# A second Strassen step in the q product of an attention block, with its statistics on another engine

## The chip, the cores and the metric

The kernel runs on one core of a Trainium2 chip. The metric is the device time of one execution in microseconds (us): 2830.47 us is the median of three runs before the change (2829.81 to 2830.92).

Five engines matter. TensorE multiplies matrices; the profile calls it PE, and its weight loads PEld. VectorE is DVE, ScalarE is ACT, GpSimd is POOL, and SyncE (SP) issues most transfers. SBUF is the memory that all of them read; PSUM holds what PE writes, in eight banks of 128 partitions by 512 float32 numbers. All data here is float32, and PE then leaves two records (instructions) for each multiply.

## The reference

Eight samples of 512 channels by 1024 positions go through two layers.

```python
# layer 0: group norm (32 groups), 8 heads of 64 channels
qkv = einsum('oc,bchw->bohw', qkv_w, group_norm(x)) + qkv_b
attn = softmax(einsum('bhnd,bhmd->bhnm', q, k) / sqrt(64))
x = x + proj_w @ (attn @ v) + proj_b
# layer 1: one norm over the whole sample, one head of 512 channels
n = (x - mean(x)) * rsqrt(var(x) + eps) * gamma + beta
q, k, v = wq @ n + bq, wk @ n + bk, wv @ n + bv
attn = softmax(q^T k * 512**-0.5)
x = x + wo @ (v @ attn^T) + bo
```

## The kernel before

**Algebra.** In layer 1 the kernel multiplies the weights beforehand: `wqk1` is wk transposed times wq, `wvo1` is wo times wv, each scaled by gamma on its way in. So a sample needs one product "q" (512 by 512 times 512 by 1024), one product "v", scores against x itself, and values. The norm is not applied to x (`untaken`, L350): q is scaled per row by gamma, gets a per-row term `norm.c` that holds mean and deviation, and the softmax gets a factor.

**Strassen.** Large products are done in Strassen's form with seven products instead of eight (`strassen`, L414): A11 B11, A12 B21, S1 T1, S2 T2, S3 T3, A22 T4, S4 B22, where S1 to S4 are sums of weights' quarters and T1 to T4 are differences of the moving operand's quarters (`Combined.make`, L394, one DVE operation of 128x1024 each). A "line" bank in PSUM takes A11 B11, S2 T2, S3 T3 and A22 T4 one upon the other; ACT copies it out in between. A "single" bank takes the other three. Some products get a second step (`by_two_steps`, L545, in layer 0's q and k and in layer 1's v): the products A12 B21, S1 T1, S4 B22 and A22 T4 are themselves done in seven, on quarters of quarters, for two row blocks together. Their weights' sums are made once (`WeightTwice`, L514), stored in DRAM and loaded for each sample by ACT's queue; the moving sums of a quarter are three DVE operations (`quarters_b`, L504: one of 128x512, L494, and two of 128x256, L500).

**Order.** For PE, ACT and DVE the order of instructions is the order of the program (`manual_schedule`), written out by hand: a generator yields after each step of PE, `together` (L607) alternates two generators, and `at_steps` (L619) calls the hooks of a step after it. POOL and SP are ordered by the framework. Tiles come from pools: 36 tiles of 128x1024 in SBUF, and in PSUM two tiles each of the tags "s" and "o", each of two banks; a new tile waits until the last reader of an old one is done.

**One sample** takes about 347 us of PE. The stages around the change are:

1. Layer 0's scores and values, in 64 units, then q and k of the next sample (`pairs_qk_twice`, L846). Its hooks divide layer 0's output by the softmax's sums: steps 18 and 19 call `divide_at` (L1108), which is `divide` (L978, one DVE operation of 128x512, L980). There are two head pairs ("couple") and two halves of the positions for each. T1 of the projection needs both halves of a pair; the second product needs both pairs' first halves.
2. The projection, `project` (L1211) in `layer0`: plain Strassen, two generators c = 0, 1 in turn, ten steps. `done` adds PSUM and the copy (L1231), adds bias and x into x (L1217), and calls `norm.of_half` (L318, a DVE statistics operation, 128x512). Four aggregates follow (L321).
3. The q stage, `make_q` (L1288) in `attention1`: plain Strassen, ten steps of PE. DVE adds (L1292), ACT scales by gamma and adds `norm.c` (L1296). Hooks make T1 to T4 of x (L400), the halved quarters of B21, T1, B22 and T4 (`halve_b`), and the norm: `mean_of_all` (L325) is a small PE product that averages over partitions (L299), a reduction (L301) and three small DVE operations (L329 to L333); `deviation` (L335) is a second small product and a power on POOL (L339). ACT's queue issues the load of `wvo1`'s sums (L523, L524).
4. The v stage (`make_v_twice`), then scores, softmax and values of layer 1.

Before the samples there is a prologue, in which weights are multiplied, scaled by gamma (`scale_rows`, L232, on ACT) and summed (`finish`, L186, L194).

The projection's second product reads what DVE divides in hooks 18 and 19 of the stage before it, and its T1 is finished there too (`combine2`, L1030):

```python
18: [lambda g=g: divide_at(couple[0], g) for g in range(2)],
19: [
    lambda: divide_at(couple[1], 0), lambda: combine2(1, 1),
    lambda: divide_at(couple[1], 1),
],
```

Of the kernel before, what the change touches and what calls it, by code (L numbers as in the profile page):

```python
# [37 lines left out]
FP = mybir.dt.float32  # L38
AF = mybir.ActivationFunctionType
# [7 lines left out]
P = 128  # L47
# [18 lines left out]
def two_attention_blocks(  # L66
# [12 lines left out]
    vectors: bass.AP,  # L79
    out: bass.AP,  # L80
# [118 lines left out]
    class Weight:  # L199
# [36 lines left out]

        def finish(self):
            for parts, rest in zip(self.parts, self.rest):
                finish(parts, rest)
            stored[self.name] = dram.tile([P, W_SIZE], FP, tag=self.name, name=f"stored_{self.name}")  # L240
            nc.sync.dma_start(stored[self.name], self.tile)
# [62 lines left out]
    class Norm:  # L304
# [19 lines left out]

        def mean_of_all(self):  # L325
            self.mean = self.average(self.stat[:, 0, :], f"m_{self.name}")
            spread = self.spread = self.tile("spread", NC)
            if self.width == 1:
                nc.vector.tensor_scalar(spread, self.stat[:, 0, :], self.mean, None, ALU.subtract)  # L329
            else:  # L330
                nc.vector.tensor_tensor(spread, self.stat[:, 0, :], self.mean, ALU.subtract)
            nc.vector.tensor_tensor(spread, spread, spread, ALU.mult)
            nc.vector.tensor_tensor(spread, spread, self.stat[:, 1, :], ALU.add)  # L333
# [177 lines left out]

    PAIRS = [[("A12", "B21"), ("S1", "T1")], [("S4", "B22"), ("A22", "T4")]]

    class WeightTwice:  # L514
# [3 lines left out]
        def __init__(self, name, make=None):  # L518
# [7 lines left out]
            for n, pair in enumerate(PAIRS):  # L526
                for i, (a, _) in enumerate(pair):
                    sums_a(self.quarters(a, make), tiles[n][:, i * 4 * P : (i + 1) * 4 * P])
            stored[key] = dram.tile([P, 16 * P], FP, tag=key, name=f"stored_{key}")
            for n in range(2):  # L530
                nc.sync.dma_start(stored[key][:, n * 8 * P : (n + 1) * 8 * P], tiles[n])
# [375 lines left out]
    def layer0(bs, qs, ks, b, norm_next):  # L907
# [5 lines left out]
        if norm_next is not None:  # L913
            for n in range(NC):
                hooks[n + 4] = [lambda cc=n, half=half: norm_next.of_half(cc, half) for half in range(2)]
            hooks[8] = [lambda cc=cc: norm_next.of_channels(cc) for cc in range(NC)]
        twice_b = {}
# [264 lines left out]
        if not last:  # L1182
# [12 lines left out]
                18: [lambda g=g: divide_at(couple[0], g) for g in range(2)],  # L1195
                19: [
                    lambda: divide_at(couple[1], 0), lambda: combine2(1, 1),
# [11 lines left out]
        later = []  # L1209

        def project(w, c):  # L1211
            def done(i, half, bank, u):
# [3 lines left out]
                def add():  # L1216
# [3 lines left out]
                    norm.of_half(chunk, half)  # L1220
# [29 lines left out]
        at_steps(  # L1250
            together(project(w, 0), project(w, 1)),
            {} if last else {2 * n - 3: [lambda n=n: combine2(n, 1)] for n in range(2, 5)},
        )
        for cc in range(NC):
            norm.of_channels(cc)
        if last:
            held(invs.pop(end), f"inv_0_{b}_{end}_1")
        return xs, norm, qs_next, ks_next

    def attention1(xs, norm, b, at_values):  # L1260
# [11 lines left out]
        w = next_weight().parts[0]  # L1272
        twice_w = []
        combine, later = Combined(f"1_{b}"), []
        combine.take(xs)
# [3 lines left out]
        twice_a, twice_b = {}, {}  # L1279
# [5 lines left out]
        def halve_b(name):  # L1285
            twice_b[name] = quarters_b(bs[name], tile2(f"{name}_twice_{b}"))

        def make_q(c):  # L1288
            def done(i, half, bank, u):
                n, to = c + 2 * i, piece(qs, c + 2 * i, half)  # L1290
                if u is not None:
                    nc.vector.tensor_tensor(u, bank, u, ALU.add)  # L1292
                    bank = u

                def scaled():
                    nc.scalar.activation(  # L1296
                        to, bank, AF.Identity, bias=norm.c[:, n : n + 1],
                        scale=vec[:, V_NW1 + n : V_NW1 + n + 1],
                    )

                if i == half == 0:
                    later.append(scaled)
                else:
                    scaled()

            return strassen(by_channels(w, c, bs), done, f"q_1_{b}_{c}")

        at_steps(together(make_q(0), make_q(1)), {
            0: [lambda: combine.make(1)],
            1: [lambda: combine.make(2)],  # L1310
            2: [norm.mean_of_all, lambda: combine.make(3)],
            3: [lambda: halve_b("B21")],
            4: [norm.deviation, lambda: combine.make(4)],
            6: [lambda: halve_b("T1")],
            7: [lambda: halve_b("B22")],
            8: [lambda: halve_b("T4")],
            5: [lambda: twice_w.append(WeightTwice("wvo1")), norm.untaken, lambda: later.pop(0)(), lambda: later.pop(0)()],
# [395 lines left out]
    made, throughs = {}, []  # L1713


    with tc.manual_schedule(engines={PE, ACT, DVE}):
# [12 lines left out]
        norm = norm0(xs_next, 0)  # L1729

# [23 lines left out]
        def through_q():  # L1754
            throughs.append(Through(wqk1, bias_q, nk1, "q", room("rows_q", 0)))
            wqk1.scale_rows(V_NW1)

        def channels_of(half, ccs):
# [25 lines left out]
            7: [wqk1.finish], 8: [waiting[0].finish], 9: [lambda: WeightTwice("qk02", both_of(w))],  # L1784
# [4 lines left out]
        for b in range(B):  # L1789
            if 0 < b < B - 1:  # L1790
                ahead = [norm0(load_x(b + 1, nc.sync), b + 1)]
            xs, norm, qs, ks = layer0(bs, qs, ks, b, ahead[0] if b + 1 < B else None)
# [15 lines left out]
            attention1(xs, norm, b, at_values)  # L1808
# [412 lines left out]
```

## Time and profile before

| | |
|---|---|
| median of 3 runs | 2830.47 us (2829.81 to 2830.92) |
| the profiled execution: its time | 2829.01 us |
| its span, first to last instruction | 2827.3 us |
| ACT busy, POOL busy | 1101.6 us, 273.7 us |
| DVE busy in the projection (939.2 to 963.8 us) and in q (963.8 to 988.3 us) of one sample | 17.78 and 18.90 us |
| ACT busy in the same two stretches | 3.52 and 8.61 us |

The profile is one execution. A row names the line, the engine, the operation, what it writes and reads, the shape and the count; then the time busy and the mean of one in ns; then the idle time of its engine before it and what ended that. A row of the view in order of time begins with the start in us and the length. Consecutive matmuls overlap in the records, since their length includes the way through the array: the distance of two starts is what one costs. The chain that ended last is followed back from the last instruction, at each step to what released it.

### The profile page before, as it was taken

What the parts mean: (1) busy time and instruction counts of PE and PEld (TensorE: products, weight loads), DVE (VectorE), ACT (ScalarE), POOL (GpSimd) and SP (SyncE); (2) the same over time, 40 slices, a digit from 0 to 9 for tenths busy, and PEclk for the clock granted to TensorE, in tenths of its full rate; (3) what the DMA queues carried; (4) which work ended last, traced back from release to release, by engine and by line L of the source; (5) the groups of instructions that cost most, each with busy time, mean ns of one, the idle gap of its engine ahead of it and who ended that gap; (6) DMA issues with size and microseconds to landing.
All of it is one profiled execution on the core that took longest, in us unless ns stands there. A gap on an engine that the chain in (4) does not pass through costs nothing.

```text
span 2827.3 us, 38614 instructions
## 1 busy us (share of the span) xinstructions
PE 2814.0 (100%) x15496; PEld 1550.4 (55%) x15496; DVE 2123.9 (75%) x2979; ACT 1101.6 (39%) x1536; POOL 273.7 (10%) x236
## 2 busy tenths in 40 slices
PE   9999999999999999999999999999999999999999
PEld 5434765357643476445773456734567346673365
DVE  6677696767867778776777777777777777767877
ACT  3462324623256232552325522265232642326432
POOL 0000220003100040000400004000040000400011
PEclk9999999999999999999999999999999999999999
DMA  8422131321323213133131331313213142121001
GB/s 288 168 74 89 53 126 64 87 90 53 112 68 91 84 67 105 59 91 109 56 108 44 89 108 56 108 49 96 96 62 103 49 119 72 64 91 52 8 16 39
DMA packets 81125, 237.76 MB, mean 84 GB/s; under 512 B 21513, under 2 KB 22313, under 8 KB 74537
## 3 DMA queue, kind: packets, MB, share of 16 engines
q1 hardware_dynamic: 73336, 208.44, 22.5%
q10 hardware_dynamic: 7600, 26.77, 2.9%
q8 instruction: 124, 2.03, 0.3%
q14 instruction: 65, 0.52, 0.1%
HBM read 179.37 MB, written 31.98 MB: 75 GB/s over the span
## 4 chain that ended last, share of the span: by engine, by line
PE 92%; DVE 6%; issue 1%; ACT 0%; SPq 0%; DMA 0%; POOL 0%; DVEq 0%; ACTq 0%; POOLq 0%
PE s L941 15%; PE ps_o L960 15%; PE ps_q L632 8%; PE ps_v L647 7%; PE ps_o L1540 7%; PE ps_p L632 6%; PE ps_l_qk L869 5%; PE ps_l L1376 4%; PE ps_s L1359 4%; PE ps_s_qk L862 4%; PE ps_l_v L647 3%; PE ps_s L1376 3%; PE ps_o_qk L862 3%; PE ps_s_v L890 2%; PE ps_s_two L1670 2%; PE ps_o_v L890 1%
## 5 line engine op out<-in xcount | busy, mean ns | idle before, releaser
L798 ACT ACTIVATE p<-s 128x1024 f32<-128x1024 f32 x512 | 523.8, 1025 | 329.0 <-PE s L941 322.2
L800 DVE TENSOR_TENSOR acc<-acc,p 128x1024 f32<-128x1024 f32 x384 | 469.6, 1223 | 101.2 <-ACT p L798 93.0
L960 PE MATMUL ps_o<-p,v 64*64 64x512 f32 x4096 | 528.6, 589 | 0.0
L941 PE MATMUL s<-c_q,c_k 64*64 64x512 f32 x3584 | 465.0, 590 | 0.0
L960 PEld LDWEIGHTS ps_o<-p,v 64*64 64x64 f32 x4096 | 156.6, 133 | 282.9 <-issue 278.0
L941 PEld LDWEIGHTS s<-c_q,c_k 64*64 64x64 f32 x3584 | 134.7, 133 | 253.2 <-issue 236.1
L339 POOL TENSOR_TENSOR rstd<-rstd,minus_half 128x4 f32<-128x4 f32 (+1 forms) x16 | 19.8, 1239 | 2076.9 <-DVE rstd L338 2076.9
L1540 PE MATMUL ps_o<-t_p,s_v 128*128 128x512 f32 x384 | 168.2, 594 | 0.0
L800 DVE TENSOR_TENSOR acc<-p,p 128x1024 f32<-128x1024 f32 x64 | 78.3, 1224 | 79.8 <-ACT p L798 79.8
L1350 ACT ACTIVATE p<-p,factor 128x512 f32<-128x512 f32 (+1 forms) x112 | 85.3, 780 | 115.7 <-DVE p L1386 91.2
L1540 PEld LDWEIGHTS ps_o<-t_p,s_v 128*128 128x128 f32 x384 | 72.3, 190 | 91.3 <-issue 89.2
L1364 ACT COPY p<-ps_s 128x512 f32<-128x512 f32 x96 | 53.1, 588 | 177.0 <-PE ps_s L1359 177.0
L1386 DVE TENSOR_TENSOR p<-ps_l,p 128x512 f32<-128x512 f32 x136 | 90.1, 684 | 40.5 <-PE ps_l L1376 40.2
L632 PE MATMUL ps_q<-t,w_wqk 128*128 128x512 f32 x256 | 116.0, 597 | 0.0
L632 PE MATMUL ps_p<-t_p,w_p 128*128 128x512 f32 x256 | 112.6, 592 | 0.5 <-DVE inv L812 0.5
L425 ACT COPY u_v<-ps_v 128x512 f32<-128x512 f32 x48 | 28.1, 586 | 204.9 <-PE ps_v L647 170.5
L1386 DVE TENSOR_TENSOR p<-ps_s,p 128x512 f32<-128x512 f32 x112 | 74.8, 685 | 37.9 <-PE ps_s L1376 37.9
L647 PE MATMUL ps_v<-w_v,t_again 128*128 128x256 f32 x448 | 99.0, 379 | 0.0
L425 ACT COPY u_q<-ps_q 128x512 f32<-128x512 f32 x54 | 31.2, 578 | 160.6 <-PE ps_q L632 160.6
L647 PEld LDWEIGHTS ps_v<-w_v,t_again 128*128 128x128 f32 x448 | 85.1, 190 | 11.6
L632 PE MATMUL ps_p<-o,w_p 128*128 128x512 f32 x192 | 88.5, 597 | 2.3 <-DVE o L980 2.3
L647 PE MATMUL ps_v<-w_v,x 128*128 128x256 f32 x384 | 86.8, 379 | 0.0
(463 smaller groups left out, 4851.1 us busy)
## 6 DMA issues: line engine op xcount, KB each, us to landing
x<-in_x SPq DMA_DIRECT2D x92, 512.0 KB, 6.4
w_qk<-stored_qk SPq DMA_DIRECT2D x14, 1792.0 KB, 7.2
w_wqk<-stored_wqk SPq DMA_DIRECT2D x8, 1792.0 KB, 7.2
fold<-acc SPq DMA_DIRECT2D x56, 256.0 KB, 3.1
qk_twice<-stored_qk_twice ACTq DMA_DIRECT2D x28, 512.0 KB, 5.8
w_wvo<-stored_wvo SPq DMA_DIRECT2D x8, 1792.0 KB, 7.4
out<-x SPq DMA_DIRECT2D x28, 512.0 KB, 4.6
w_v<-stored_v SPq DMA_DIRECT2D x7, 1792.0 KB, 7.0
```

What stands on the lines that cost most here:

```text
L632: nc.tensor.matmul(bank, w[a][:, k, c * P : (c + 1) * P], bs[b][:, k, :], start=fresh and k == 0, stop=k == 1, skip_group_check=True,)
L647: nc.tensor.matmul(bank[:, u * 2 * P : (u + 1) * 2 * P], bs[b][:, k, n * P : (n + 1) * P], w[a][:, k, :], start=fresh and u == k == 0, sto ...
L798: nc.scalar.activation(p, s, AF.Exp, scale=factor)
L800: nc.vector.tensor_tensor(acc, first, p, ALU.add)
L862: nc.tensor.matmul(bank[:, i * 2 * P : (i + 1) * 2 * P], parts[a][x], twice_b[v][y], start=start and i == 0, stop=True, skip_group_check=True,
L869: nc.tensor.matmul(bank, of(i, a)[:, k, :], bs[v][:, k, :], start=start and k == 0, stop=k == 1, skip_group_check=True,)
L941: nc.tensor.matmul(s[cols, j, :], ks[pair][k0 // HALF][rows, k0 % HALF : k0 % HALF + HD], qs[pair][g][rows, :], start=True, stop=True,)
L960: nc.tensor.matmul(o[cols, half, :], vs[kt][rows, c0 : c0 + HD], p[rows, j, :], start=kt == 0, stop=kt == NT - 1,)
L1359: nc.tensor.matmul(bank, bs[v][:, k, t * P : (t + 1) * P], q_parts[a][:, k, :], start=a == "A11" and k == 0, stop=k == 1, skip_group_check ...
L1376: nc.tensor.matmul(bank[:, u * 2 * P : (u + 1) * 2 * P], v[y][:, u * P : (u + 1) * P], a[x], start=start and u == 0, stop=True, skip_group ...
L1386: nc.vector.tensor_tensor(at(r, t), bank, at(r, t), ALU.add)
L1540: nc.tensor.matmul(bank, v_parts[kt // 2][a][:, kt % 2, c * P : (c + 1) * P], p_parts[kt // 2][b][:, kt % 2, cols], start=fresh and kt == ...
```

## The change

1. **Layer 1's q gets the second Strassen step.** For each row block r = 0, 1 the line takes A11 B11, S2 T2 and S3 T3 only; the four other products are done as quarter products, in two pairs: (A12 B21, S4 B22) and (S1 T1, A22 T4). The two lines of A11 B11 stand before and between the first three quarter products.
2. **The weights are scaled by gamma on both sides** in the prologue, by DVE (`scale_both`), so that ACT need not scale q; a new input `gamma1` is loaded as a row to all partitions. The sums for `wqk1` are made in four steps, as hooks of layer 0's v stage of the first sample, stored, and loaded for each sample in the projection's first hook.
3. **Statistics of x by ACT.** `of_half` and `of_channels` go. Each half of a channel chunk gets two passes of ACT that sum over 512 positions: the mean, and the square about the first half's mean. Seven small POOL operations put the two halves together; the three small operations after the mean go from DVE to POOL.
4. **The halvings of B22 and B21** move from the q stage into the projection's last steps.
5. **The quotients' order**: both pairs' first halves at step 18, the second halves at step 19.

```diff
+        def scale_both(self, by, row):
+            for cc in range(NC):
+                for to, a in self.moving(cc):
+                    nc.vector.scalar_tensor_tensor(
+                        a, a, vec[:, by + cc : by + cc + 1], row[:, to], ALU.mult, ALU.mult
+                    )
...
+        def pass_over(self, cc, half, name, func, **args):
+            to = onepool.tile([P, HALF], FP, tag="held", name=f"{name}_{self.name}_{cc}_{half}")
+            nc.scalar.activation(to, piece(self.xs, cc, half), func, **args)
+
+        def moments(self, cc, half, first):
+            mean, part = self.stat[:, 0, cc : cc + 1], self.part[:, cc, 0 if first else 1, :]
+            self.pass_over(
+                cc, half, "mean", AF.Identity, scale=1.0 / HALF,
+                accum_out=mean if first else part[:, 1:2],
+            )
+            self.pass_over(
+                cc, half, "square", AF.Square, bias=mean, scale=-1.0, accum_out=part[:, 0:1]
+            )
+
+        def both_halves(self):
+            mean, var = self.stat[:, 0, :], self.stat[:, 1, :]
+            (q0, q1), d = (self.part[:, :, i, 0] for i in range(2)), self.part[:, :, 1, 1]
+            nc.gpsimd.tensor_tensor(d, d, mean, ALU.subtract)
+            nc.gpsimd.tensor_tensor(q0, q0, q1, ALU.add)
...
         def mean_of_all(self):
             self.mean = self.average(self.stat[:, 0, :], f"m_{self.name}")
             spread = self.spread = self.tile("spread", NC)
+            engine = nc.gpsimd if self.width == 1 else nc.vector
...
+    PAIRS_Q = [[("A12", "B21"), ("S4", "B22")], [("S1", "T1"), ("A22", "T4")]]
...
-                18: [lambda g=g: divide_at(couple[0], g) for g in range(2)],
+                18: [lambda pair=pair: divide_at(pair, 0) for pair in couple],
                 19: [
-                    lambda: divide_at(couple[1], 0), lambda: combine2(1, 1),
+                    lambda: divide_at(couple[0], 1), lambda: combine2(1, 1),
                     lambda: divide_at(couple[1], 1),
                 ],
...
-                    norm.of_half(chunk, half)
+                    if i == half or i == 1:
+                        norm.moments(chunk, half, i == half)
+                    if (i, half, c) == (1, 0, 1):
+                        ready.halve("B21")
...
+        hooks[0] = [ready.load]
+        hooks[7] = [lambda: ready.halve("B22")]
+        at_steps(together(project(w, 0), project(w, 1)), hooks)
-        for cc in range(NC):
-            norm.of_channels(cc)
...
+        def make_q(w):
+            parts = ready.weights.all(columns_of(w))
+            first, second = ([tile2(f"{n}_q_1_{b}_{r}") for r in range(2)] for n in ["c11", "c22"])
+            lines = [banks("o", f"ps_l{r}_q_1_{b}")[:, 0, :] for r in range(2)]
+
+            def pair(products, to, name):
+                line, single = (banks("s", f"ps_{name}{n}_q_1_{b}")[:, 0, :] for n in range(2))
...
+                for bank, x, y, start, use, r, t in [
+                    (line, "A11", "B11", True, nc.scalar.copy, 0, 0),
+                    (single, "A12", "B21", True, add, 0, 0),
+                    (line, "S2", "T2", False, nc.scalar.copy, 0, 1),
+                    (single, "S1", "T1", True, nc.scalar.copy, 1, 1),
+                    (line, "S3", "T3", False, add, 1, 1),
+                    (single, "S4", "B22", False, add, 0, 1),
+                    (line, "A22", "T4", False, nc.scalar.copy, 1, 0),
+                ]:
+                    for i, (a, v) in enumerate(products):
+                        nc.tensor.matmul(
+                            bank[:, i * 2 * P : (i + 1) * 2 * P], parts[a][x], twice_b[v][y],
+                            start=start and i == 0, stop=True, skip_group_check=True,
+                        )
...
+            yield from line(0, "A11", "B11", True)
+            yield from some(quarters, 2)
+            yield from line(1, "A11", "B11", True)
+            for n in range(5):
+                next(quarters)
+                if n == 0:
+                    take(0)
+                if n == 4:
+                    take(1)
+                yield
+            yield from line(0, "S2", "T2", False)
+            yield from line(1, "S2", "T2", False)
+            quarters = pair(PAIRS_Q[1], second, "s")
+            for n in range(7):
+                next(quarters)
+                if n == 2:
+                    c12_of(0)
+                if n == 4:
+                    c12_of(1)
+                yield
...
+            for r in range(2):
+                multiply(r, "S3", "T3", False)
+                for n, half in enumerate([1, 0]):
+                    final(r, 1, half, lines[r], second[r][:, n, :])
+                yield
+
+        at_steps(make_q(w), {
+            1: [lambda: norm.moments(0, 1, False)],
+            2: [lambda: combine.make(1), lambda: norm.moments(1, 1, False)],
+            3: [lambda: combine.make(2), norm.both_halves],
+            6: [lambda: combine.make(4)],
+            8: [lambda: twice_w.append(WeightTwice("wvo1"))],
+            9: [norm.mean_of_all, lambda: ready.halve("T1")],
+            10: [norm.deviation, lambda: ready.halve("T4")],
+            12: [lambda: combine.make(3)],
+            14: [norm.untaken],
         })
...
+        gamma_row = tile2("gamma_row")[:, 0, :]
+        nc.sync.dma_start(gamma_row, gamma1.to_broadcast([P, C]))
...
-            wqk1.scale_rows(V_NW1)
+            wqk1.scale_both(V_NW1, gamma_row)
...
+                lambda: WeightTwice("qk02", both_of(w)), lambda: WeightTwice("wqk1", columns_of(wqk1), over),
```

`add`, `take` (C11), `c12_of` (C12) and `final` are DVE operations of 128x512 that read PSUM and a tile in SBUF, except the two `final` calls after the last quarter products, which read two tiles in SBUF. The list `over` holds the four steps of sums for `wqk1`; layer 0's v stage of the first sample calls them at its steps 0 to 3.

## The prediction

> **What bounds the kernel now.** I read the page's busy times first, then the chain that ended last, then who waited for whom on the matrix engine (PE), then the instructions in order of time around one layer-1 q stage.
>
> ```profile
> span 2827.3 us, 38614 instructions
> PE 2814.0 (100%) x15496; PEld 1550.4 (55%) x15496; DVE 2123.9 (75%) x2979; ACT 1101.6 (39%) x1536; POOL 273.7 (10%) x236
> PEclk9999999999999999999999999999999999999999
> PE 92%; DVE 6%; issue 1%; ACT 0%; SPq 0%; DMA 0%; POOL 0%; DVEq 0%; ACTq 0%; POOLq 0%
> ```
>
> PE is busy all the time, at an undivided clock, and is 92% of the chain. So only two things shorten this kernel: fewer matrix products, or the few waits that PE has. The reverse is the danger: PE has hardly a wait to lose and many to gain.
>
> The next lines are PE in order of time, around the projection (L1217's stage) and the q stage of one sample. A start minus the one before it is what PE needs.
>
> ```profile
> 939.19 2.74 PE L632 MATMUL ps_p<-o,w_p 128*128 128x512 f32 x6
> 942.26 2.41 PE L632 MATMUL ps_p<-o,w_p 128*128 128x512 f32 x5 [0.33 <-DVE o L980]
> ...
> 963.82 7.03 PE L632 MATMUL ps_q<-x,w_wqk 128*128 128x512 f32 x16
> 970.69 1.88 PE L632 MATMUL ps_q<-t,w_wqk 128*128 128x512 f32 x4
> ```
> ```profile
> 341.77 1.03 PE L1376 MATMUL ps_l<-spare 128*128 128x256 f32 x4
> 342.63 1.03 PE L1376 MATMUL ps_s<-spare,B_twice 128*128 128x256 f32 x4
> 343.50 1.03 PE L1376 MATMUL ps_s<-spare 128*128 128x256 f32 x4
> 344.52 1.13 PE L1376 MATMUL ps_l<-spare,B_twice 128*128 128x256 f32 x4
> ```
>
> A multiply leaves two records. Sixteen records of 512 columns take 970.69 - 963.82 = 6.87 us, 0.429 each; four of 256 columns take 0.865, 0.216 each. Halving the columns halves the price, so a second Strassen step saves its full eighth. Two waits stand in these lines. At 942.26 PE waited for a division on VectorE (DVE): six records from 939.19 end at 941.77, so 0.49, and the record after the wait follows at 0.53 instead of 0.43, 0.10 more. At 344.52 it is 0.16 before and 0.10 after: PE works again from 344.62, and its DVE releaser had ended at 344.46. So a result is of use to PE only if it is there 0.16 us before the product's turn; I use that below.
>
> **The change, term by term, for one sample.**
>
> *Products.* The q stage has 28 multiplies of 512 columns, 56 records: 56 x 0.429 = 24.02 us. Afterwards it has 12 of them for the lines (24 records, 10.30) and 28 of 256 columns (56 records, 12.10): 22.40. **-1.62.** The two small products for mean and variance stay.
>
> *Quotients' order.* Dividing both pairs' first halves first puts what the second product reads at 940.3, ahead of its turn at 940.91. The 0.6 us above go; what is late next on DVE (division of second halves, T1) is not read before 946. **-0.6**, in seven samples; the last has another path.
>
> *What becomes late.* PE now arrives 0.6 earlier at stages where DVE and ScalarE (ACT) have more to do in front of it. I laid each engine's instructions end to end in their new order from 939.19, with the durations of these rows, DVE and ACT in order. The same bookkeeping of the old order lands within 0.03 us of the rows of this sample.
>
> ```profile
> 955.44 0.59 ACT L425 COPY u_p<-ps_p 128x512 f32<-128x512 f32 x1 [1.13 <-PE ps_p L632]
> 957.15 0.59 ACT L425 COPY u_p<-ps_p 128x512 f32<-128x512 f32 x1 [1.13 <-PE ps_p L632]
> ```
> ```profile
> 956.06 0.69 DVE L1231 TENSOR_TENSOR u_p<-ps_p,u_p 128x512 f32<-128x512 f32 x1 [5.13 <-ACT u_p L425]
> 956.78 0.75 DVE L1217 SCALAR_TENSOR_TENSOR x<-u_p,bias,x 128x512 f32<-128x512 f32 x1
> 957.57 0.69 DVE L318 BATCH_NORM_STATS2 part<-x 128x6 f32<-128x512 f32 x1
> 958.18 0.67 DVE L1231 TENSOR_TENSOR u_p<-ps_p,u_p 128x512 f32<-128x512 f32 x1
> ```
>
> A statistics pass has no row. Bounds: 0.59 (the copies from PSUM above) and 0.81 (L372, two per-partition operands). L1350 with one such operand takes 0.72, so one costs 0.09; I take 0.63 for the mean's pass and 0.72 for the square's, plus 0.09 each for reading the accumulator (the pace at L808: 0.58 against 0.49). A pair is 1.5 us, 12 us a sample on ACT; DVE sheds eight L318 (0.6 each).
>
> - The second chunk's copy now queues on ACT behind the first chunk's two passes, and those wait for DVE. At the projection's start that puts the copy from 945.14 to 946.6, and PE's fourth step waits 0.23.
> - At its end the copy goes from 957.15 (0.6 less by the gain) to 958.7, and DVE sits 2.2 us idle before its next add. Behind that stand the moved halvings of B22 and B21 (0.68 + 2 x 0.42, 1.5 each, L494 and L500). The add that frees the PSUM tile for the first q line ends at 963.65, PE wants it at 963.46: 0.35. The second line's tile is late by 0.21.
> - The quarter products use two banks in turn. A bank's turn is 0.19 (drain) + 0.59 copy + 0.16 = 0.94, or 1.04 with an add (0.69), against a product of 0.865: 0.07 and 0.18, in each of the two pairs. T3 stands ahead of such adds in the second pair: together 0.07 + 0.18, and 0.07 + 0.16 + 0.07 + 0.36.
> - The last two adds on q end 1.6 us after PE; the v stage reuses those tiles 1.8 and 2.7 us after, so nothing.
>
> Sum 1.70. Sample: -1.62 - 0.60 + 1.70 = **-0.52**. With passes at 0.59 it is -0.85, at 0.72 and 0.81 it is -0.15.
>
> *GpSimd's ten small operations* (seven for both halves, three for the spread) replace DVE's aggregates and three ops. No row has a four-element add. Bounds: below, 0.1 (a memset of one element); above, 1.02 (L339 on four elements). The adds of 256 and 512 elements take 0.73 and 1.27, a line that meets four elements at 0.20: I take that. The first seven have 2.6 us to spare. The three stand between the two small products, and beside them DVE halves T1:
>
> ```profile
> L339 POOL TENSOR_TENSOR rstd<-rstd,minus_half x16: 1017/1210/1472, 29.5 to 2692.4; 128x4 f32<-128x4 f32 x8, 128x1 f32<-128x1 f32 x8
> L1347 POOL TENSOR_TENSOR acc<-acc,p x48: 1259/1711/2362, 354.0 to 2777.0; 128x512 f32<-128x512 f32 x48
> L1429 DVE TENSOR_TENSOR p<-p,p x32: 1217/1832/2153, 336.7 to 2765.3; 128x1024 f32<-128x1024 f32 x32
> ```
>
> Same shapes, spread of almost two: the two engines hold each other up. The one-element power takes 1.47 beside a DVE operation, the four-element one 1.02 alone. If each of the three waits out one DVE operation, the variance's product is 0.53 late and the quarters behind it 0.25: +0.78 a sample. If they slip between: 0. I take 0, as the excess on the smallest row (0.45) is under the DVE time beside it (1.05), and keep 0.78 for the range.
>
> The Trainium skill speaks against the change here: GPSIMD Engine Reference, section Specifications, has the SBUF interfaces shared with VectorE, with contention when a DVE instruction has two SBUF inputs. The halvings have two, L1386 with one from PSUM stays at 0.67 to 0.69 beside GpSimd. By that page alone the sum would be the higher one, 2833.7.
>
> *Once.* Scaling the weights goes from ACT to DVE: eight of about 0.4 (half of 0.75, L664's form, and its fixed part) at 45.7, where T3 and, later, a q add were due; 0.2 + 0.4 of PE, and the sums over four steps lie in a stage where DVE idles 6 us at a time: **+0.7** (0 to 3). The two loads of 512 KB a sample on ACT's queue issue beside the first passes and have 20 us to land in 5; stores and gamma's row on SP's queue are once. Nothing there.
>
> **Sum.** 7 x -0.52, last sample -0.1 (no quotient gain, but less lateness), +0.7: -3.0. The profiled execution took 2829.0, its span 2827.3; the median is 2830.5. So **2827.5**.
>
> **Rivals.**
> 1. *The lateness is absorbed* (0.27). Every wait but the banks' turns is a few tenths; shorter passes or an earlier add erase them. Then 0.57 remains (0.07 + 0.18, and 0.07 + 0.07 + 0.18): -1.65 x 7 - 1.05 + 0.7 = -11.9, **2818.6**. For it: DVE sheds 5 us of L318. Against: it idles behind ACT.
> 2. *The variance's chain over GpSimd* (0.22). Place: between the two small products, PE queued behind with all second quarters. At 0.2 an operation with the hold-up +0.26 a sample, 2833.7; each 0.1 more costs 0.3. From 0.35 us an operation it is slower by over 0.2%; at 0.5 the mean is late too, +1.56 a sample, **2844**. A third of this case lies inside 0.2%.
> 3. *Square is not in the loaded table* (0.05). The trace has one table load, 1.28 us, for Identity, Copy and Exp. Two loads a sample before the passes and before Exp, the first at the projection's start: up to 1.28 each of PE, **2837**. The Trainium skill, ScalarE: Activation LUTs, section Table sets, names relu, copy, identity and abs as in every set, but not square; no row here shows it.
>
> Forecast 0.42, other mishaps 0.04. About 0.2% (5.7 us) is what a measurement of this kernel can tell from no change. Faster by more: rival 1 and the low tail of the forecast, 0.34. Slower by more: two thirds of rival 2, rival 3, 0.18. Same: 0.48. Range 2817.5 to 2838: it takes in rival 1 and the hold-up, and leaves out rival 2's far end.
>
> **What would show it.** The q stage from its first record to v's first: 23.8 us where it was 24.5 (963.82 to 988.30) if right, 23.1 by rival 1, over 24.5 by rival 2. PE's start at the projection without the gap at 942. Statistics passes of 0.6 to 0.75; GpSimd's small operations at 0.2, and the second small product without a wait on them. A second table load anywhere, or PE waiting on ACT's copies in the projection for over half a microsecond, would make it wrong.

## The result, and the profile after

The changed kernel takes **2838.47 us** (median of 7 runs, 2837.35 to 2840.36) where the kernel before takes 2830.47 in the same 7 rounds: the ratio is 1.0029, with a 95% interval of 1.0020 to 1.0039. It is slower by 8.0 us. The forecast was 2827.5, and the time lies half a microsecond above the range.

The page of the changed kernel, with the lines that answer to those of before: span, busy times, and the engines' shares of the chain that ended last.

```profile
span 2838.6 us, 39373 instructions
...
PE 2817.4 (99%) x15688; PEld 1582.2 (56%) x15688; DVE 2136.5 (75%) x2963; ACT 1166.5 (41%) x1752; POOL 299.3 (11%) x316
...
PE 85%; DVE 9%; DMA 3%; ACT 1%; issue 1%; SPq 0%; ACTq 0%; DVEq 0%
```

PE's share of the chain falls from 92% to 85%, and VectorE (DVE) and DMA take it over: what ends last is no longer products alone. Part of the DMA share is a false lead: the chain puts 29.0 us on the transfer of `w_wvo`, and E12 below shows that the gap is not its doing. The next view is PE in order of time, through the projection of the sample that the prediction worked on, up to the first q line.

```profile
941.89 7.03 PE L679 MATMUL ps_p<-o,w_p 128*128 128x512 f32 x16
948.75 1.88 PE L679 MATMUL ps_p<-t_p,w_p 128*128 128x512 f32 x4
951.49 10.57 PE L679 MATMUL ps_p<-t_p,w_p 128*128 128x512 f32 x24 [0.85 <-DVE u_p L1284]
...
967.36 1.98 PE L679 MATMUL ps_l_q<-x,w_wqk 128*128 128x512 f32 x4 [0.15 <-DVE u_p L1284]
```

Sixteen records start without a break at 941.89: the gap of before (942.26, the division) is gone. But from 948.75 four records need 1.72 us, and the next one starts 2.74 us later: 1.02 us are lost there and 0.10 more on the record behind (the restart, in the words below). The new wait is nearly twice the old one. It stands at the step that the prediction counts as the projection's fourth; the texts below call it the third. Its releaser is an add on DVE. DVE in order of time, same stretch:

```profile
941.70 0.68 DVE L1030 TENSOR_TENSOR o<-o,inv 128x512 f32<-128x512 f32 x1
943.04 0.69 DVE L1030 TENSOR_TENSOR o<-o,inv 128x512 f32<-128x512 f32 x1 [0.66 <-DMA inv<-inv_rows]
...
946.89 0.68 DVE L1284 TENSOR_TENSOR u_p<-ps_p,u_p 128x512 f32<-128x512 f32 x1
947.61 0.75 DVE L1267 SCALAR_TENSOR_TENSOR x<-u_p,bias,x 128x512 f32<-128x512 f32 x1
950.74 0.69 DVE L1284 TENSOR_TENSOR u_p<-ps_p,u_p 128x512 f32<-128x512 f32 x1 [2.38 <-ACT u_p L461]
```

The division of the second pair, which the change moved ahead, stands 0.66 us idle until the transfer of its inverse has landed. All that is behind it on DVE comes later, the add of the first chunk (946.89) too. And ScalarE (ACT):

```profile
948.46 0.63 ACT L335 ACTIVATE mean<-x 128x512 f32<-128x512 f32 x1 [4.07 <-DVE x L1267]
948.99 0.19 ACT L335 ACTIVATION_READ_ACCUMULATOR mean<-x 128x1 f32 x1
949.21 0.72 ACT L335 ACTIVATE square<-x,stat 128x512 f32<-128x512 f32 x1
949.27 0.32 ACTq L560 DMA_DIRECT2D wqk_twice<-stored_wqk_twice  x1
949.69 0.39 ACTq L561 DMA_DIRECT2D wqk_twice<-stored_wqk_twice  x1
949.84 0.19 ACT L335 ACTIVATION_READ_ACCUMULATOR square<-x,stat 128x1 f32 x1
950.12 0.58 ACT L461 COPY u_p<-ps_p 128x512 f32<-128x512 f32 x1
```

The first chunk's passes wait for that late add, and the second chunk's copy stands behind both passes and behind two issues of loads. When it starts (950.12), PE has been through with the bank that it reads since about 947.2 (twelve records and the drain from 941.89); the add of 950.74 waits for the copy, PE for the add. So a late transfer reaches PE by way of DVE, ACT and DVE again, each of which works in order.

The stages, sample by sample, from PE's first starts in each (us). "Start" is when the first projection begins, which takes in the prologue; "last" is the last sample from its projection to the last product. Ranges are over the first seven samples, a number in brackets is one that stands out. The rows of the experiments are for the next section.

| kernel | start | projection | q | last | median |
|---|---|---|---|---|---|
| before | 245.5 | 24.63 | 24.48 | 168.5 | 2830.47 |
| changed | 246.4 | 25.31 to 25.80 | 24.38 | 172.5 | 2838.47 |
| E1 before, new order alone | 245.0 | 24.03 | 24.48 | 168.7 | 2824.99 |
| E2 changed, old order | 246.9 | 24.95 (25.71) | 24.38 | 170.6 | 2834.09 |
| E3 changed, inverses in halves | 245.9 | 24.71 to 24.74 | 24.38 (24.73) | 172.3 | 2834.40 |
| E4 changed, passes behind copies | 245.5 | 24.03 (24.22) | 24.12 | 169.4 | 2825.47 |
| E5 changed, statistics on DVE | 246.7 | 24.13 | 26.17 | 172.3 | 2841.32 |
| E6 changed, spread on DVE | 245.7 | 24.73 to 25.80 | 24.43 | 173.0 | 2840.96 |
| E7 changed, halvings late | 246.7 | 25.04 to 25.30 | 24.14 | 171.2 | 2833.97 |
| E8 = E4, and the last sample | 246.0 | 24.03 (24.61) | 24.12 | 168.5 | 2823.62 |
| E9 = E8, T1 halved earlier | 246.6 | 24.03 | 23.85 | 168.1 | **2821.70** |
| E10 = E9, inverses in halves | 246.4 | 24.03 | 23.84 (24.19) | 167.9 | 2822.82 |
| E11 = E4, old order | 245.8 | 24.63 (25.30) | 24.12 | 171.2 | 2829.10 |
| E12 changed, loads a step later | 246.2 | 25.08 to 26.14 | 24.38 | 171.1 | 2838.61 |

In E2, E8, E11 and E12 one sample has a transfer so late that PE waits for the division that needs it, 0.20 to 0.37 us, in either order; these are the projections that stand out there (25.71, 24.61, 25.30, 26.14).

The profiled execution of the changed kernel took 2840.35, 11.3 more than that of before: 0.9 by the first projection, 6.3 in seven samples (0.57 to 1.18 each), 4.0 in the last. Of the last 4.0, 1.7 are a stretch at a lower granted clock that other executions of both kernels also have or lack (see the last section).

### The profile page after: what moved, and what is told of

Read it like the earlier page. It is cut to its first block, busy times and chain, and to the rows that moved or that the text cites. A ratio compares the mean times of both kernels' runs of the same rounds, so it can differ in the third digit from the quotient of the medians.

```text
span 2838.6 us, 39373 instructions
## 1 busy us (share of the span) xinstructions
PE 2817.4 (99%) x15688; PEld 1582.2 (56%) x15688; DVE 2136.5 (75%) x2963; ACT 1166.5 (41%) x1752; POOL 299.3 (11%) x316
## 4 chain that ended last, share of the span: by engine, by line
PE 85%; DVE 9%; DMA 3%; ACT 1%; issue 1%; SPq 0%; ACTq 0%; DVEq 0%
PE s L991 15%; PE ps_o L1010 15%; PE ps_o L1674 7%; PE ps_v L694 7%; PE ps_l_qk L916 4%; PE ps_l L1510 4%; PE ps_s L1493 4%; PE ps_s_qk L909 3%; PE ps_l_q L679 3%; PE ps_l_v L694 3%; PE ps_s L1510 3%; PE ps_o_qk L909 3%; PE ps_s_v L937 2%; PE ps_s_q L1373 2%; PE ps_p L679 2%; PE ps_s_two L1804 2%
## 5 line engine op out<-in xcount | busy, mean ns | idle before, releaser
L352 POOL TENSOR_TENSOR part<-part,stat 128x4 f32<-128x4 f32 x8 | 3.6, 454 | 1443.6 <-ACT mean L335 1443.6
L1284 DVE TENSOR_TENSOR u_p<-ps_p,u_p 128x512 f32<-128x512 f32 x48 | 33.0, 687 | 76.5 <-ACT u_p L461 76.5
L679 PEld LDWEIGHTS ps_p<-t_p,w_p 128*128 128x128 f32 x256 | 48.0, 190 | 72.7 <-issue 54.2
```

The lines of the kernel that those rows point to most:

```text
L679: nc.tensor.matmul(bank, w[a][:, k, c * P : (c + 1) * P], bs[b][:, k, :], start=fresh and k == 0, stop=k == 1, skip_group_check=True,)
```

## The experiments

Theory T: the moved division waits for a transfer; the wait becomes PE's because passes and loads stand on ACT ahead of a copy. Rivals: R1, the passes alone make the gap; R2, the loss is GpSimd's chain in the q stage; R3, the transfer's wait reaches PE by DVE alone. Each kernel was timed in turn with the kernel before on the same chip, and the ratios are to that (its medians there lay between 2829.59 and 2830.15).

### E1 to E4: the order, the transfer, the passes

**E1**, the kernel before with the new order of divisions and nothing else.

```diff
-                18: [lambda g=g: divide_at(couple[0], g) for g in range(2)],
+                18: [lambda pair=pair: divide_at(pair, 0) for pair in couple],
...
-                    lambda: divide_at(couple[1], 0), lambda: combine2(1, 1),
+                    lambda: divide_at(couple[0], 1), lambda: combine2(1, 1),
```

> The kernel before with the quotients' order alone. Theory T (the moved division of the second pair waits 0.5 to 1.0 us for the transfer of its inverse, and this reaches PE only because ACT's statistics passes stand between DVE's add and the next copy): the gap of 0.6 us at the second product goes in seven samples, VectorE shows the wait for the transfer, but the next PSUM tile comes at most 0.1 to 0.2 us late, so about -3 us: 2827.0 to 2828.0. Rival R1 (the transfer's wait is absorbed everywhere, the passes alone make the gap): -4.2 us, 2826.3. Rival R3 (the transfer's wait reaches PE by VectorE alone): gain and loss cancel, 2830 to 2831.

Measured: 2824.99, ratio 0.9982 (0.9973 to 0.9991). DVE and PE of this kernel in order of time:

```profile
938.50 0.69 DVE L980 TENSOR_TENSOR o<-o,inv 128x512 f32<-128x512 f32 x1 [0.51 <-DMA inv<-inv_rows]
```
```profile
937.50 7.03 PE L632 MATMUL ps_p<-o,w_p 128*128 128x512 f32 x16
944.37 12.18 PE L632 MATMUL ps_p<-t_p,w_p 128*128 128x512 f32 x28
```

DVE waits for the transfer here too, yet PE runs the whole projection without a gap: 24.03 instead of 24.63 in all seven samples. So R3 falls for waits of this size (0.44 to 0.88 us here), and with statistics on DVE the transfer's wait is wholly absorbed (T had allowed 0.1 to 0.2 us of it; R1's 2826.3 was the nearer number). The seven samples give the 4.2 us, and the two profiled executions differ by no more; the other 1 us of the medians is not explained.

**E2**, the changed kernel with the old order (the same edit backwards).

> The changed kernel with the old quotients' order. T: the gap of 0.6 us at the second product returns, the wait of VectorE for the transfer and the gap of 0.8 to 1.3 us at the third step go; projection 25.05 us where it was 25.3 to 25.8, so -3.7 us: 2834.3. R1 (passes alone): the second gap only shrinks by what PE comes later, net nothing: 2838. R2 (the loss is in the q stage, by GpSimd's chain): 2838 or above.

Measured: 2834.09, ratio 1.0014 (1.0005 to 1.0023). PE in one projection:

```profile
1289.28 2.74 PE L679 MATMUL ps_p<-o,w_p 128*128 128x512 f32 x6
1292.35 4.56 PE L679 MATMUL ps_p<-o,w_p 128*128 128x512 f32 x10 [0.33 <-DVE o L1030]
1296.74 3.60 PE L679 MATMUL ps_p<-t_p,w_p 128*128 128x512 f32 x8
```

The old gap is back and the new one gone, as T has it (24.95, and 2834.3 expected). The order alone is worth 5 us off in one kernel and 4 us on in the other.

**E3**, the changed kernel, in which the transfers that spread the second couple's inverses are split, and the first halves of both pairs go first.

```diff
+                for half in range(2):
+                    for n, pair in enumerate(couple):
+                        for j in range(2):
+                            cols = slice(half * HALF, (half + 1) * HALF)
+                            queues[j].dma_start(
+                                spreads[pair][j * HD : (j + 1) * HD, half, :],
+                                rows[2 * n + j : 2 * n + j + 1, cols].to_broadcast([HD, HALF]),
+                            )
```

> The changed kernel with the inverses of the second couple sent in halves, the first halves of both pairs ahead of the second halves (eight transfers of 128 KB for four of 256 KB). T: VectorE's wait for the transfer goes, PE's gap at the third step of the projection falls from 0.8-1.3 to 0.2-0.3 us, so -5.3 us: 2832.7. R1 (passes alone): gap and time stay, 2838.

Measured: 2834.40 (2832.15 to 2835.49), ratio 1.0013 (1.0004 to 1.0022). DVE, where the two divisions stand in one row:

```profile
940.09 1.28 DVE L1030 TENSOR_TENSOR o<-o,inv 128x512 f32<-128x512 f32 x2
```

They follow each other without a wait, and PE's loss at the third step is 0.27 and 0.10 where it was 1.02 and 0.10. The projection takes 24.7, as T said; only the transfers were changed, so R1 falls. The seven samples are 5.4 us shorter than in the changed kernel's profile, which is T's 5.3. The median came 1.7 us above T's number; why is not shown.

**E4**, the changed kernel, in which the first chunk's passes are issued behind the second chunk's copy (first and second pair of sums of the projection, all samples but the last's first).

```diff
+                while behind:
+                    behind.pop(0)()
...
-                        norm.moments(chunk, half, i == half)
+                        behind.append(lambda: norm.moments(chunk, half, i == half))
+                    if c == 1 or i != half or last and i == 0:
+                        while behind:
+                            behind.pop(0)()
```

> The changed kernel with the first chunk's statistics passes issued behind the second chunk's copy from PSUM (in the projection's first and second pair of sums; not in the last sample's first). T and R1: PE's gap at the third step goes although VectorE still waits for the transfer: -7.4 us, 2830.6, and down to 2827.5 if VectorE's idle time of 2.2 us ahead of the q stage goes too and with it the waits on the q lines' PSUM tiles. R2: 2838.

Measured: 2825.47, ratio 0.9983 (0.9974 to 0.9992). ACT in order of time:

```profile
942.90 0.58 ACT L461 COPY u_p<-ps_p 128x512 f32<-128x512 f32 x1 [2.85 <-PE ps_p L679]
944.34 0.63 ACT L335 ACTIVATE mean<-x 128x512 f32<-128x512 f32 x1 [0.85 <-DVE x L1269]
```

The copy now waits for PE and not for passes. DVE and PE:

```profile
938.92 0.69 DVE L1030 TENSOR_TENSOR o<-o,inv 128x512 f32<-128x512 f32 x1 [0.87 <-DMA inv<-inv_rows]
```
```profile
937.55 7.03 PE L679 MATMUL ps_p<-o,w_p 128*128 128x512 f32 x16
944.42 12.18 PE L679 MATMUL ps_p<-t_p,w_p 128*128 128x512 f32 x28
```

PE runs the projection without a gap (24.03; 24.22 in one sample), although DVE still waits for the transfer, 4.7 us over the seven samples where the changed kernel has 5.3. The waits on the two q lines are gone as well (q 24.12), since DVE no longer sits idle behind ACT before them; that is the lower end of what T allowed, and 2 us below it. R2 falls: 13 us came back without a touch on GpSimd's chain.

### E5 to E8: statistics, spread, halvings, the last sample

**E5**, the changed kernel with the statistics back on DVE (`norm.of_half` for every half, `norm.of_channels` at the q stage's step 3, no passes).

```diff
-                    if i == half or i == 1:
-                        norm.moments(chunk, half, i == half)
+                    norm.of_half(chunk, half)
```

> The changed kernel with the statistics of x back on VectorE (one 128x512 statistics operation for each half of a chunk and four aggregates, as before; the small operations after the mean stay on GpSimd). T: without passes on ScalarE the copies are no longer late, the gap of 0.8 to 1.3 us at the projection's third step goes in seven samples (-7.4 us) although VectorE waits for the transfer as before; but eight operations of 0.6 us now stand ahead of the adds that free the q lines' tiles, up to 1 us of PE a sample: 2831 to 2837. If the passes are no cause (the transfer alone): 2838 or slower.

Measured: 2841.32, ratio 1.0039 (1.0025 to 1.0053). PE:

```profile
949.95 12.18 PE L679 MATMUL ps_p<-t_p,w_p 128*128 128x512 f32 x28
...
972.22 1.98 PE L679 MATMUL ps_l_q<-x,w_wqk 128*128 128x512 f32 x4 [1.29 <-DVE u_p L1283]
```

The gap of the projection goes (24.13), which T said. But the second q line waits 1.46 us for the add that frees its PSUM tile, and a quarter product 0.63: q takes 26.17. T's price for DVE, up to 1 us a sample, was too low by nearly half (1.8). The time alone would fit the other case (2838 or slower); the missing gap speaks against it. In this order DVE cannot carry the statistics beside the second step's extra adds; whether it could in another was not run.

**E6**, the changed kernel with the three small operations after the mean on DVE (`engine = nc.vector`).

> The changed kernel with the three small operations between the two small products on VectorE as before; the seven for both halves stay on GpSimd. T: the wait of 0.17 us and its restart of 0.06 at the second small product go, but T4's halving comes 0.3 to 0.5 us later and may cost as much: 2836.2 to 2839. Rival 2 of the prediction (the variance's chain over GpSimd is the main loss): -6 us or more, below 2832.

Measured: 2840.96, ratio 1.0039 (1.0025 to 1.0052). PE:

```profile
980.54 0.28 PE L307 MATMUL ps_v<-spread,in_sample 128*128 128x4 f32 x2
980.68 1.98 PE L1373 MATMUL ps_s_q<-t,w_wqk 128*128 128x256 f32 x8
982.50 1.10 PE L1373 MATMUL ps_s_q<-T_twice,wqk_twice 128*128 128x256 f32 x4
983.84 1.35 PE L1373 MATMUL ps_s_q<-T_twice,wqk_twice 128*128 128x256 f32 x5 [0.24 <-DVE c_q L1361]
```

The second small product no longer waits, but an add that stands behind T4's halving on DVE is now late, and a quarter product loses 0.41 where it lost 0.08: q is 24.43, no gain. The time is also 1.3 us longer outside the span (2840.96 against 2837.9 in the profiled execution, 3.1, and 2.6 to 2.8 in its other runs, where the others have 1.7 to 1.9), which no row explains and which puts it above T's 2839; by the spans E6 is within 2 us of the changed kernel. R2 falls again.

**E7**, the changed kernel with the halvings of B22 and B21 behind the projection's last add.

```diff
-        hooks[7] = [lambda: ready.halve("B22")]
         at_steps(together(project(w, 0), project(w, 1)), hooks)
+        ready.halve("B22")
+        ready.halve("B21")
```

> The changed kernel with the halvings of B22 and B21 behind the projection's last add on VectorE. T: the waits at the first two q lines (0.42 and 0.25 us a sample) go, at most 0.3 comes back where the first pair's third quarter product needs the halved quarters: 2833 to 2835.5. If these adds are late through ScalarE's copies and not through the halvings: 2838.

Measured: 2833.97, ratio 1.0013 (1.0003 to 1.0022). The first two q lines start without a wait, and 0.07 and 0.10 come back at the first halved quarter: projection and q together 49.2 to 49.4 where they were 49.7 to 50.2. So part 4 did cost what the prediction put on it, but not by itself: in E4 the same waits go with the halvings left where they were, so it takes both the halvings and the late copies.

**E8**, E4 with the last sample mended too: there the second chunk's passes are held back until both copies of the second sums are issued.

```diff
-                    if c == 1 or i != half or last and i == 0:
+                    if (c == 0 if last and i == half == 0 else c == 1 or i != half):
...
+        if last:
+            hooks[5] = [flush]
```

> The kernel with the passes behind the copies, and in the last sample the second chunk's passes held back until both copies of the second sums are issued. T: the wait of 1.16 us with its restart in the last sample's projection goes: 2824.3 where the passes-behind kernel took 2825.5. If that wait has another cause: 2825.5.

Measured: 2823.62, ratio 0.9978 (0.9969 to 0.9987). The last sample's projection falls from 27.37 to 26.51; before, 26.11.

### E9 and E10: a version that beats both kernels

**E9**, E8 with the first operation of T1's halving one step earlier, ahead of the mean's small product.

```diff
-            8: [lambda: twice_w.append(WeightTwice("wvo1"))],
-            9: [norm.mean_of_all, lambda: ready.halve("T1")],
+            8: [lambda: twice_w.append(WeightTwice("wvo1")), lambda: ready.halve_first("T1")],
+            9: [norm.mean_of_all, lambda: ready.halve_rest()],
```

> The kernel of the run before (passes behind the copies, last sample too) with the first operation of T1's halving put ahead of the mean's small product. T: GpSimd's three small operations after the mean no longer stand beside VectorE's 128x512 operation, so they fall from 0.66, 0.26 and 0.38 us towards 0.2 each, and the wait of 0.17 us with its restart of 0.06 at the second small product goes: -1.8 us, 2821.8. If their length has nothing to do with VectorE: 2823.6.

Measured: **2821.70** (2820.64 to 2823.22), ratio 0.9972 (0.9962 to 0.9983). GpSimd in the changed kernel, and then in this one:

```profile
973.66 1.21 POOL L354 TENSOR_SCALAR part<-part 128x4 f32<-128x4 f32 x1
...
979.83 0.66 POOL L365 TENSOR_SCALAR spread<-stat,mean_m 128x4 f32<-128x4 f32 x1 [4.00 <-DVE mean_m L309]
980.57 0.26 POOL L368 TENSOR_TENSOR spread<-spread 128x4 f32<-128x4 f32 x1
980.91 0.38 POOL L369 TENSOR_TENSOR spread<-spread,stat 128x4 f32<-128x4 f32 x1
```
```profile
967.78 1.19 POOL L352 TENSOR_TENSOR part<-part,stat 128x4 f32<-128x4 f32 x1 [170.00 <-ACT mean L335]
969.06 0.24 POOL L354 TENSOR_SCALAR part<-part 128x4 f32<-128x4 f32 x1
...
974.33 0.43 POOL L365 TENSOR_SCALAR spread<-stat,mean_m 128x4 f32<-128x4 f32 x1 [4.08 <-DVE mean_m L309]
974.85 0.27 POOL L368 TENSOR_TENSOR spread<-spread 128x4 f32<-128x4 f32 x1
975.19 0.20 POOL L369 TENSOR_TENSOR spread<-spread,stat 128x4 f32<-128x4 f32 x1
```

Without the 128x512 operation of DVE beside them the three take 0.90 and not 1.30 (the two halvings of 128x256 still are), and the second small product starts on time: q 23.85. Of the seven operations before, it is now the first that stands beside a DVE operation of 128x1024 (L352, 1.19, in the changed kernel 0.39) and no longer the second. T's number was 2821.8.

**E10**, E9 with E3's split transfers.

> The same kernel with the first halves of both pairs' inverses sent ahead of the second halves as well. T: the waits of VectorE for that transfer go; with the passes behind the copies they reach PE only where the transfer is over 1 us late (0.1 to 0.6 us in one or two samples of a run), so -0.3 to -0.8 us against the kernel without it, about 2821.3. If the eight transfers cost their queues more than they bring: 2822 or more.

Measured: 2822.82, ratio 0.9974 (0.9965 to 0.9984): not better, and the 1.1 us to E9 lie within the spread of either's runs. In these two profiles the transfer's wait does not reach PE (projection 24.03 with and without it).

### E11 and E12: order against passes, and the loads' issue

**E11**, E4 with the old order.

> The kernel with the passes behind the copies, with the old quotients' order. T: once no pass stands ahead of the copy, the new order is worth its whole gap of 0.6 us in seven samples, so undoing it costs 4.2 us: 2829.7, where undoing it with the passes ahead of the copy brought 4 us. If the wait for the transfer made the new order bad in itself: 2825.5 or less.

Measured: 2829.10, ratio 1.0000 (0.9990 to 1.0009); T said 2829.7. With E2, E4 and the changed kernel this makes a square: passes ahead of the copy, new order 2838.5 and old 2834.1; passes behind it, new 2825.5 and old 2829.1. Order and passes cannot be priced one by one.

**E12**, the changed kernel with the load of the sums issued behind the second chunk's copy.

```diff
-        hooks[0] = [ready.load]
+        hooks[1] = hooks.get(1, []) + [ready.load]
```

> The changed kernel with the load of wqk's sums issued on ScalarE's queue one step later, behind the second chunk's copy. T: the two issues take 0.32 and 0.39 us in ScalarE's order between the square's pass and the copy, and the copy starts 0.28 us after the accumulator's read where it starts 0.09 after it elsewhere: PE's gap falls by 0.2 us in seven samples, -1.3 us, about 2836.8. If these issues wait for the landing of w_wvo, as the chain that ended last has it: the copy no longer waits for the landing, the gap goes, -6 us, about 2832.

Measured: 2838.61, ratio 1.0030 (1.0018 to 1.0041): the median shows nothing. The trace does. ACT:

```profile
948.24 0.72 ACT L335 ACTIVATE square<-x,stat 128x512 f32<-128x512 f32 x1
948.87 0.19 ACT L335 ACTIVATION_READ_ACCUMULATOR square<-x,stat 128x1 f32 x1
948.96 0.56 ACT L461 COPY u_p<-ps_p 128x512 f32<-128x512 f32 x1
```

The copy starts 0.09 after the read and not 0.28, and PE's idle time is the transfer's wait less 0.02, where it was the wait plus 0.19, in six of the seven samples (in the other DVE waited at both divisions, and PE at the first one too). That share of the gap is the loads' issue; the chain's "DMA w_wvo" ahead of them is not their releaser, since the gap did not go. In the profiled executions the seven projections are 177.4 us in sum where the changed kernel has 179.0, about T's gain; why the median does not show it stays open.

## Where the prediction was right and wrong

**The failed step** is "Dividing both pairs' first halves first puts what the second product reads at 940.3", with "what is late next on DVE (division of second halves, T1) is not read before 946". I laid the engines' instructions end to end and let a moved one start when its engine was free. Its operand was not there. In seven samples of the changed kernel DVE's wait for the transfer and PE's idle time behind it were (us):

| sample | 0 | 1 | 2 | 3 | 4 | 5 | 6 |
|---|---|---|---|---|---|---|---|
| DVE waits for the inverse | 0.77 | 0.65 | 0.66 | 0.50 | 0.99 | 0.84 | 0.90 |
| PE idle at the third step | 0.97 | 0.84 | 0.85 | 0.70 | 1.18 | 1.03 | 1.09 |

Always 0.19 to 0.20 more. By E4 the wait costs next to nothing where no pass stands ahead of the copy: so what failed is the time of that operand, and then the overlap of the lateness behind it with ACT's passes. The trace of before would have told the first. The row of these transfers there, in the view of the line that issues them:

```profile
L1100 SPq DMA_DIRECT2D inv<-inv_rows x42: 476/562/598, 187.3 to 2321.8; - x42
...
DMA to landing us min/median/max: 3.5/5.2/6.0
```

In the sample of the prediction the last of the four was issued at 934.2 or so on ACT's queue (two in 933.36 to 934.73); with 5.2 to 6.0 us it lands at 939.4 to 940.2, and the moved division would have started at 939.6.

**The gap at the third step**, forecast as 0.23. By start-to-start differences it is 1.22 on average (0.35 and 0.10 more than the transfer's wait): 0.76 the transfer, 0.20 the loads' issue on ACT, which I had put at nothing beside the passes, and 0.25 the passes with PE's restart. This split follows the rows one behind the other and is not a price list: without the transfer's wait 0.37 is left (E3), without the passes ahead of the copy nothing (E4). So the passes were priced about right, and two terms were missing. Seven times 0.96 is 6.7 of the 11 us between forecast and measurement; GpSimd and the last sample (below) hold most of the rest.

**The other waits** came close, per sample: first q line 0.42 (0.35 forecast), second 0.25 (0.21), first pair's banks 0.33 (0.25), second pair 0.57 (0.66). E7 and E4 confirm the two causes of the first two, the halvings and the late copies. My 23.8 us for q didn't follow from my own terms (24.48 - 1.62 + 0.21 + 0.25 + 0.66 is 23.98); measured 24.38.

**The products** were right: 24 records of 512 columns and 56 of 256. In E9, with the waits on the lines and on the second small product gone, q is 0.63 shorter: the 1.62 less the 1.0 of waits that are left.

**GpSimd.** 0.20 for a small operation was right (0.20 to 0.22 where no DVE operation with two SBUF inputs is beside it). The hold-up, which I took as 0, is real: the same operation takes 1.21 beside such an operation of 128x1024 and 0.24 beside one that reads PSUM, and the second small product is 0.23 late, 1.8 us in all. I had put the hold-up, if it came, at 0.78 a sample: rival 2 had the right place, at a price more than three times too high. The Trainium skill's GPSIMD Engine Reference, section Specifications, which has the SBUF interfaces shared in just this case, agrees with these rows, but gives no size. The 2833.7 that I put beside it would have come nearer to the measurement by luck.

**Once.** The first projection starts at 246.4 in the changed kernel against 245.5; over all traces 245.5 to 246.9 with the changed prologue and 245.0 and 245.5 without. About 1 us, 0.7 forecast.

**The last sample** was set at -0.1 and cost 2.3 (4.0 less the clock's 1.7): both chunks' passes, four in a row, stood ahead of a copy (1.16), and in q a copy stood behind four passes, which themselves started 0.74 late behind the pass over the inverse (L855) that only this sample has there (0.63). I didn't lay its order out.

**Rivals.** 1 (lateness absorbed) was wrong as the change stands and right once the passes stand behind the copies. 2 is treated above. 3 is out: the trace has one table load (1.28 us), as before, with the square passes in it; the Trainium skill's ScalarE: Activation LUTs, section Table sets, had left that open. Slower by more than 0.2% is what came, and I had given it 0.18 (my own terms, two thirds of rival 2 and rival 3, make 0.20). That the range nearly holds the time is luck: its upper part stands for GpSimd's hold-up and for table loads, and neither is the main loss. The signs I named would have told: PE waits over half a microsecond on what ACT's copies release.

## What to carry to other kernels

When an instruction is moved ahead on an engine that works in order, look up when each of its operands is there, and for a transfer that means its issue plus its landing row; then ask who stands behind it. Work given to an idle engine is not free where short operations that others wait for share its queue: put it behind them (here 13 us of 2838 by order alone). Prices of two edits that meet in one queue don't add, so try them together and apart.

## What the runs showed of the hardware

**The granted clock after a short wait.** In the last sample's v stage PE waits 2.1 us for DVE, in every kernel. In six of the fourteen profiled executions the products behind it then run at half speed for a while. The view by stretches of the changed kernel; the columns are length, PE, PEld, DVE, ACT, POOL busy, PE clock, DMA share and GB/s:

```profile
2731.00:2736.00 5.00, 4.55 (x13) 3.70 (x14) 2.28 (x4) 0.00 (x0) 2.95 (x4) 0.66 0.00 0
2736.00:2741.00 5.00, 5.00 (x22) 4.01 (x22) 2.64 (x5) 0.00 (x0) 0.96 (x1) 1.00 0.00 0
```

Eight records of 256 columns take 0.427 us each instead of 0.216: 1.7 us, where the seven runs of the changed kernel spread over 3.0. The Trainium skill's TensorE: Matmul & The Clock Gate, section "What's actually happening", ties a lower clock to an idle window of about 3.4 us; here it follows a wait of 2.1 us at times.

**Reading ACT's accumulator** is a record of 0.19 us that overlaps the pass by 0.10. Another pass over x starts 0.22 after the read's start, a copy 0.09 after it. The 0.22 is not the read's own price: the passes at L855 that read `ps_o_qk` follow each other at 0.09 too. They write another tile, while the passes over x share one; that this makes the difference is not shown. A pair of passes over x therefore takes 1.60 us ahead of another such pass and 1.47 ahead of a copy, where 1.53 was forecast.

**Issuing a load on ACT's queue** takes its place in ACT's order: two issues (0.32 and 0.39) run beside a pass of 0.72, and what is over holds the next instruction back by 0.19.
